# Layer 1's front as a pipeline over four steps, and layer 0's token totals placed behind later products

## The chip, the cores and the metric

The kernel runs on one core of one Trainium2 chip. The metric is the device time of one execution in microseconds; lower is better. A core has five engines that run side by side, each through its own queue of instructions in order: TensorE (PE, matrix products; its weight loads are shown apart as PEld), VectorE (DVE), ScalarE (ACT), GpSimd (POOL) and SyncE (SP), which here issues most of the DMA transfers. GpSimd issues the gathers, DMA transfers whose rows are picked by a list of indices.

## The reference

Four layers run one after the other on 2048 tokens of 512 numbers. Each layer mixes a token block with a per-request 64x64 matrix (or a like condition) and then runs a network; the result is added to x. The change touches the fronts of the first two:

```python
x = x + _L0_ffn_ref(_L0_cond_ref(x, ...), ...)   # attention, shared expert, 7 experts, the best 2 of each token
x = x + _L1_ffn_ref(_L1_cond_ref(x, ...), ...)   # 32 experts, the best 4 of each token
...
# layer 0, the experts
shared = expert_ffn(x, sh_gate, sh_up, sh_down)
probs = jax.nn.sigmoid(x @ router_w + router_b)
scores, idx = jax.lax.top_k(probs, 2)
...
return shared + combined
# layer 1, mixing and the choice of experts
w = weights[subjects]
out = jnp.einsum('bct,bcd->bdt', x, w)
...
logits = x @ gate_w.T + gate_b
topk_logits, topk_idx = jax.lax.top_k(logits, 4)
```

## The kernel before

The 2048 tokens are 16 tiles (`NT`) of 128 rows. Everything is float32 apart from small one-hot tables.

**Layer 0's front** (`layer0`, `Front`) runs 16 steps. In each, the list `turns` (L465) calls the stages in a fixed order, each for the tile that lies `lag` steps back, and `g.held` pins all instructions in that order on every engine. Two tiles at a time are entered in the lists of their experts by `Moe.put` (L1152), a generator with five parts: one-hot marks on VectorE; two products `at` on TensorE; places on VectorE; two float16 tables `a_` and `b_` (the second of two scalings is on ScalarE); and `total` (L1140), four products of the tables on TensorE and an add into `tokens` on VectorE. `front` (L863) runs parts one, three and four; `count` (L871) runs part two in odd steps and the total in even ones. After `count` come `down_rows` (the shared expert's second product), a few small stages, `qkv` and `probs_turn`.

The shared expert of tiles 6 to 12 (`LATER`) isn't done in layer 0's front. Two of these (`GAP`) are done between layer 0's experts and layer 1; the other five, tiles 8 to 12, fill TensorE during layer 1's front.

**Layer 1's front** (`Mixed.run`, L1780) finishes layer 0 and chooses layer 1's experts for each tile. For a tile: `fetch` gathers two expert rows `yk` per token (GpSimd); `adds` adds them, scaled, to x on VectorE (x of tiles 8 to 15 is loaded during the stage by `bridge.rest`); `mix` is a product with the tile's mixing matrix, copied to `c` by ScalarE and stored to `rows`; `turn` transposes c on TensorE and copies it to `cT` on ScalarE; `route` makes the logits, either in four parts on disjoint columns of the array (`SPLIT` tiles, with `partss` copied by ScalarE and summed by one more product in `logits`) or in eight products straight to `rp`; `choose` adds the bias and finds the largest values on VectorE. After tiles 3, 7, 11, 13 and 15 (`GROUPS`) a `Ranked.put` (L1504) of four or two tiles runs through five parts: VectorE, TensorE (`at`), VectorE, VectorE, TensorE (`table`).

The five shared experts are cut by `Shared.pieces` (L539) into 30 pieces: four quarters of gate and up for each tile (eight products of 128 columns), and two halves of down (one 512-column product each). When the fourth quarter is out, `act` on VectorE is kept as a late action that `acts` calls. After the second half of down, ScalarE copies the result to `sht` and GpSimd adds it to x.

In one step s of 17, the order written out by hand is: fetch(s + 6), mix(s), adds(s + 1), a piece, logits(s - 1), turn(s), late actions, choose(s - 1), a piece, the puts' next parts, route(s), a piece, a new put. So mix, turn and route of one tile follow each other on TensorE in one step, with one piece between each two. Four pieces stand ahead of step 0, and 26 in steps 0 to 8. Two PSUM buffers (tag `sh`) serve gate/up and down in turn, so a new gate/up buffer waits for the act of the tile before.

After the stage, `m.end` turns the table into the list `fixed`, by which the first expert rows are gathered for layer 1's experts.

Of the kernel before, what the change touches and what calls it, by code (L numbers as in the profile page):

```python
# [10 lines left out]
F32 = mybir.dt.float32  # L11
# [10 lines left out]
P = 128  # L22
# [19 lines left out]
FIXED1 = 2  # L42
TC1 = 96
LATER = range(6, NT - 3)
LEAD = 6
GROUPS = {3: 4, 7: 4, 11: 4, 13: 2, 15: 2}
SPLIT = range(9)
GAP = 2
EARLY = range(LATER[GAP])
BIG = 65536.0  # L50
# [374 lines left out]
def layer0(g, w3, pool3):  # L425
    tc, nc, a = g.tc, g.nc, g.a
    with ExitStack() as ctx:
        keep = ctx.enter_context(tc.tile_pool(name="l0keep", bufs=1))
        g.constants(keep, "cst01")
        clear = g.results(keep)  # L430
        xs = g.stream("x0")
        ln2 = g.load(keep, "ln2")
        m = Moe(g, ctx, keep, E0, K0, [C0] * E0, V0, "w_e0", W0, l0_expert, ln2)
        with ExitStack() as c1:
            wp = c1.enter_context(tc.tile_pool(name="l0w", bufs=1))
            sb = c1.enter_context(tc.tile_pool(name="l0sb", bufs=2))
            at0 = g.cond_rows(wp, "cond0")
            x, other = {}, {}

            def load(i):  # L440
                if i < NT:
                    x[i] = g.load_x(sb, a["x"], i, 5)

            def swapped(i):
                if i < NT:
                    other[i] = sb.tile([P, D], F32, name="xw")
                    for k in range(2):
                        r = i * P + 64 * (1 - k)
                        g.dma(other[i][64 * k : 64 * k + 64, :], a["x"][r : r + 64, :], later=False)

            load(0)
            swapped(1)
            load(1)
            load(2)
            w = {k: g.load(wp, k) for k in ("ln1", "w_lat", "w_q", "w_kn", "w_kr", "w_v", "w_o", "w_r0")}
            shared = Shared(g)
            w.update(shared.w)
            br = g.load_bcast(wp, "b_r0")
            g.at1 = g.cond_rows(wp, "cond1")
            ps = c1.enter_context(tc.tile_pool(name="l0ps", bufs=3, space=PSUM, reuse_waits="tile"))  # L460
            bank = ps.tile([P, 512], F32, name="tok", tag="tok", bufs=1)
            m.begin(sb, bank, bank[:, 256:448])
            f = Front(g, sb, ps, w, br, ln2, at0, m, x, other, xs, shared)

            turns = (  # L465
                ("mix", 0), ("copied", 0), ("values", 2), ("pair_scaled", 0), ("qk_turn", 1), ("pair_normed", 0),
                ("copied", -1), ("route", 3), ("out_turn", 2), ("gate_up", 3), ("norm_turn", 0), ("scores", 1),
                ("chosen", 3), ("pair_scaled", -1), ("latents", 0), ("softmax", 1), ("pair_normed", -1), ("weights", -2),
                ("front", 3), ("out", 2), ("summed", 2), ("count", 3), ("down_rows", 3), ("weigh", 1), ("scaled", 2),
                ("normed", 2), ("x_sum", 2), ("down_sum", 3), ("qkv", 0), ("probs_turn", 1), ("out_norm", 2),  # L470
            )
            plain, g.nc = g.nc, SimpleNamespace(**{**vars(g.held), "sync": g.nc.sync})
            for step in range(NT):
                if step:
                    clear()
                if step == 15:
                    m.weights(0)
                for stage, lag in turns:
                    if 0 <= step - lag and (lag >= 0 or step % 2 == 0):
                        getattr(f, stage)(step - lag)  # L480
                load(step + 3)
                if step % 2:
                    swapped(step + 2)
            m.weights(1)
            f.tail()
            m.end(sb)
            g.nc = plain
        m.ready(ctx)
        tot = keep.tile([P, NT], F32, name="tot0")
        nc.vector.tensor_reduce(tot, m.vals[:, :, 0:K0], AX.X, ALU.add)  # L490
        nc.vector.reciprocal(tot, tot)
        nc.vector.tensor_tensor(
            m.gates, m.vals[:, :, 0:K0], tot.unsqueeze(2).to_broadcast([P, NT, K0]), ALU.mult
        )
        w3["sb"] = ctx.enter_context(tc.tile_pool(name="l3p", bufs=1))
        bridge = Bridge(g, xs, shared)
        combined = m.run(xs, Side(g, (layer3_ahead(g, pool3, w3), bridge.work(), layer3_tables(g, w3)), w3))
        with ExitStack() as c2:
            sb = c2.enter_context(tc.tile_pool(name="gapsb", bufs=2, reuse_waits="tile"))
            ps = c2.enter_context(tc.tile_pool(name="gapps", bufs=2, space=PSUM, reuse_waits="tile"))  # L500
            todo = LATER[:GAP]
            for i in todo:
                shared.up(sb, ps, i)
            for i in todo:
                shared.down(ps, i, bridge.x[i])
        m.beyond()
        return bridge, combined


class Shared:  # L510
# [28 lines left out]
    def pieces(self, sb, ps, todo, x):  # L539
# [23 lines left out]
        def down(i, ic):  # L563
            if ic == 0:
                ys[i] = ps.tile([P, D], F32, name="y", tag="sh")
            nc.tensor.matmul(ys[i], acts[i][:, ic, :], w["w_shd"][:, ic, :], start=ic == 0, stop=ic == 1)
            if ic:
                t = sb.tile([P, D], F32, name="sht", bufs=2)
                nc.scalar.copy(t, ys[i])
                nc.gpsimd.tensor_tensor(x[i], x[i], t, ALU.add)  # L570

        on_pe = []
        for k, i in enumerate(todo):
            for q in range(4):
                if q == 2 and k:
                    on_pe += [(partial(down, todo[k - 1], ic), None) for ic in range(2)]
                on_pe.append((partial(up, i, q), partial(act, i) if q == 3 else None))
        on_pe += [(partial(down, todo[-1], ic), None) for ic in range(2)]
        return on_pe

    def down(self, ps, i, x, tag="sh"):

# [9 lines left out]
class Front:  # L592
# [276 lines left out]
            next(self.puts[0])  # L869

    def count(self, i):  # L871
        if self.puts:
            next(self.puts[0], None)
            if i % 2 == 0:
                self.puts.clear()

    def up(self, i, quarters):

# [835 lines left out]
class Mixed:  # L1714
# [17 lines left out]
    def adds(self, i):  # L1732
        if i >= NT:
            return
        g, x = self.g, self.bridge.x[i]
        for k, yk in enumerate(self.yk.pop(i)):
            g.held.vector.scalar_tensor_tensor(x, yk, self.before.gates[:, i, k : k + 1], x, ALU.mult, ALU.add)
        g.held.sync.dma_start(out=self.xs[i * P : (i + 1) * P, :], in_=x)

    def mix(self, i):  # L1740
        nc = self.g.held
        o = self.ps.tile([P, D], F32, name="mm", bufs=1)
        nc.tensor.matmul(o, self.bridge.weights[i], self.bridge.x[i], start=True, stop=True)
        self.c[i] = self.sb.tile([P, D], F32, name="c")
        nc.scalar.copy(self.c[i], o)
        nc.sync.dma_start(out=self.m.rows[i * P : (i + 1) * P, :], in_=self.c[i])
# [33 lines left out]
    def run(self):  # L1780
# [8 lines left out]
                self.late.pop(0)()  # L1789

        def fill(n=1):
            for piece, late in pieces[:n]:
                if len(pieces) <= 2:
                    acts()
                piece()
                if late:
                    self.late.append(late)
            del pieces[:n]

        def go(engine, among=None):  # L1800
            for put in list(puts if among is None else among):
                if put[1] == engine:
                    put[1] = next(put[0], None)
                    if put[1] is None:
                        puts.remove(put)

        for i in range(LEAD):
            self.fetch(i)
        fill(4)
        self.adds(0)  # L1810
        for s in range(NT + 1):
            self.fetch(s + LEAD)
            bridge.rest(self.wp, todo[0] + 2 + s)
            if s < NT:
                self.mix(s)
            if s not in SPLIT:
                go("tensor", puts[-1:])
            self.adds(s + 1)
            fill()
            if s:  # L1820
                self.logits(s - 1)
            if s < NT:
                self.turn(s)
            acts()
            if s:
                self.choose(s - 1)
            fill()
            go("tensor")
            go("vector")
            if s == NT - 1:  # L1830
                go("vector")
            if s < NT:
                self.route(s)
            fill()
            if s - 1 in GROUPS:
                puts.append([m.put(self.sb, self.ps, s - GROUPS[s - 1], GROUPS[s - 1]), "vector"])
                go("vector")
            if s in (10, 12):
                m.weights((s - 10) // 2)
        for engine in ("tensor", "vector", "vector"):  # L1840
            go(engine)
        gates = m.softmax()
        next(gates)
        go("tensor")
        assert not puts and not pieces
        m.end(self.ps)
        next(gates, None)

# [1102 lines left out]
```

## Time and profile before

| | us |
|---|---|
| median of 3 runs | 2548.62 (2548.58 to 2551.81) |
| the profiled execution | 2554.14 |
| its span, first to last instruction | 2552.3 |
| layer 0's front | up to about 362 |
| layer 0's experts and the two shared experts in the gap | to 589 |
| layer 1's front, to the token list | 589.8 to 706.1 |
| gathers `yk` in it | 32 issues, 589.95 to 661.3 |
| VectorE's scaled add of one gathered row block (128x512), median | 0.75 |
| ScalarE's copy of 128x512 | 0.59 |
| GpSimd's add of 128x512 to x | 1.27 |

A row of the timeline gives the start, the time that the merged instructions took, the engine, the line (L244 is the helper through which all pinned instructions go), the operation with the tile it writes and those it reads, the shape, and in brackets how long the engine had stood idle and what ended that. "issue" means that nothing in the profile explains the idle time, "remote" that a semaphore ended it whose sender the profile doesn't tell. A row of the waits gives an engine and tile, what it waited for, the total, how often, and the longest. Small differences of one profile (some tenths of a microsecond) are not to be read as time of the kernel.

### The profile page before, as it was taken

The numbers are of one execution on the slowest core, as the hardware profiler recorded it, in microseconds if no ns is written. First come the engines' busy times: TensorE is split into PE (matmuls) and PEld (weight loads), VectorE is DVE, ScalarE is ACT, GpSimd is POOL, SyncE is SP. The second block draws the span as 40 slices with busy tenths as digits, with TensorE's granted clock in tenths as the row PEclk, the third lists the DMA queues.
The fourth block names the chain that finished last, engine by engine and source line by source line (L and its number), as shares of the span: only waits on it lengthen the run. The fifth ranks groups of instructions, "written<-read, shape, count | busy, mean of one in ns | idle before, by whom it ended". The sixth has DMA issues, their size and how long they took to land.

```text
span 2552.3 us, 42553 instructions
## 1 busy us (share of the span) xinstructions
PE 2428.8 (95%) x16625; PEld 1622.7 (64%) x16625; DVE 1425.7 (56%) x3471; ACT 710.5 (28%) x1475; POOL 889.8 (35%) x928
## 2 busy tenths in 40 slices
PE   7999989998789999969999999999999999979998
PEld 5777766666566666747666666666666665435665
DVE  4667865733755554436544544544544432657897
ACT  2444511112211111101322222222222221246664
POOL 2122235604144443523333333333333212573440
PEclk8999999998799999989999999999999999989999
DMA  6242135526466977844222222222222213423551
GB/s 252 100 144 98 56 115 179 193 94 198 164 201 225 361 265 259 293 138 163 68 75 77 73 73 73 73 73 78 76 77 76 81 55 136 164 70 107 150 144 55
DMA packets 133850, 341.49 MB, mean 134 GB/s; under 512 B 24250, under 2 KB 25306, under 8 KB 126337
## 3 DMA queue, kind: packets, MB, share of 16 engines
q1 hardware_dynamic: 92000, 190.94, 21.7%
q0 software_dynamic: 41056, 141.89, 17.7%
q10 hardware_dynamic: 576, 5.77, 0.6%
q8 instruction: 136, 2.23, 0.4%
q14 instruction: 82, 0.66, 0.1%
HBM read 247.33 MB, written 107.22 MB: 139 GB/s over the span
## 4 chain that ended last, share of the span: by engine, by line
PE 51%; DVE 2%; POOL 1%; issue 1%; DMA 1%; ACT 0%; ACTq 0%; POOLq 0%; DVEq 0%; SPq 0%
PE out L2322 9%; PE lp L2181 8%; PE zp L2258 8%; PE pp L2637 3%; PE hp L2290 3%; PE gp L2313 3%; PE y L2886 2%; PE yp L2124 2%; PE sp L2816 2%; PE pT L2838 2%; PE op L2864 2%; PE ep L2267 1%; PE kp L2789 1%; PE out L2328 1%; PE ap L2112 1%
## 5 line engine op out<-in xcount | busy, mean ns | idle before, releaser
L1375 PE MATMUL gu<-xT,wt 128*128 128x320 f32 (+5 forms) x1536 | 397.5, 406 | 8.3 <-DVE xT L1362 7.0
L1375 PEld LDWEIGHTS gu<-xT,wt 128*128 128x128 f32 x1536 | 283.4, 192 | 121.9 <-issue 49.6
L2181 PEld LDWEIGHTS lp<-xnT,sb_mu 128*128 128x128 f32 x2048 | 236.3, 194 | 10.8 <-issue 6.7
L2181 PE MATMUL lp<-xnT,sb_mu 128*128 128x128 f32 x2048 | 239.3, 277 | 3.6 <-DVE xnT L334 2.9
L2322 PE MATMUL out<-sb_w,gT 128*128 128x512 f32 x512 | 234.9, 602 | 0.0
L2258 PE MATMUL zp<-sb_w,xnT 128*128 128x512 f32 x512 | 226.5, 592 | 0.0
L1388 PE MATMUL y<-wt,hT 128*128 128x512 f32 (+2 forms) x544 | 200.0, 595 | 1.2 <-DVE hT L1022 0.6
L362 POOL DMA_INDIRECT kvst<-kv,gidx x96 | 95.7, 997 | 263.7 <-DMA oldkv<-kvst 195.1
L2258 PEld LDWEIGHTS zp<-sb_w,xnT 128*128 128x128 f32 x512 | 93.7, 190 | 104.8 <-issue 102.4
L2322 PEld LDWEIGHTS out<-sb_w,gT 128*128 128x128 f32 x512 | 92.2, 190 | 96.1 <-issue 92.8
L362 POOL DMA_INDIRECT yk<-ys,slot x96 | 98.4, 1025 | 126.3 <-DVE pre L1484 82.0
L362 POOL DMA_INDIRECT kvt<-newkv,oidx x96 | 100.3, 1045 | 113.7 <-PE pT L2838 46.6
L2317 DVE COPY gT<-gp 128x512 f32<-128x512 f32 x64 | 44.3, 692 | 168.3 <-PE gp L2313 168.3
L1388 PEld LDWEIGHTS y<-wt,hT 128*128 128x128 f32 (+2 forms) x544 | 72.7, 166 | 63.9 <-issue 49.3
L362 POOL DMA_INDIRECT xr<-rows,stok x101 | 98.3, 973 | 37.6 <-issue 18.6
L1021 POOL TENSOR_TENSOR ga<-ga,sg 128x288 f32<-128x288 f32 (+5 forms) x66 | 50.9, 771 | 168.4 <-ACT sg L1017 167.0
L2295 ACT ACTIVATE h<-hp 128x512 f32<-128x512 f32 x128 | 73.1, 597 | 120.0 <-PE hp L2290 105.5
L2219 POOL TENSOR_TENSOR eT<-eT,inv 128x512 f32<-128x512 f32 x64 | 67.1, 1051 | 76.2 <-DVE inv L2218 70.3
L2269 ACT COPY ew<-ep 128x512 f32<-128x512 f32 x64 | 37.2, 583 | 201.9 <-PE ep L2267 201.9
L244 POOL TENSOR_TENSOR rstd<-ms,sb_cst 128x1 f32<-128x1 f32 x32 | 17.7, 554 | 210.6 <-DVE ms L244 210.6
L2186 DVE TENSOR_TENSOR lT<-lp,cmu 128x512 f32<-128x512 f32 x64 | 44.2, 690 | 81.0 <-PE lp L2181 79.1
L2827 ACT ACTIVATE s<-s,m 128x336 f32<-128x336 f32 x128 | 72.7, 569 | 46.7 <-DVE m L2823 39.4
(450 smaller groups left out, 4624.6 us busy)
## 6 DMA issues: line engine op xcount, KB each, us to landing
ys<-yo SPq DMA_DIRECT2D x106, 256.0 KB
oldkv<-kvst SPq DMA_DIRECT2D x96, 224.0 KB
kvt<-oldkv SPq DMA_DIRECT2D x96, 224.0 KB
ys<-zero SPq DMA_DIRECT2D x10, 2048.0 KB
xt<-x SPq DMA_DIRECT2D x62, 256.0 KB
x<-xt SPq DMA_DIRECT2D x48, 256.0 KB
wt<-w_e SPq DMA_DIRECT2D x7, 1536.0 KB
sb_w<-w SPq DMA_DIRECT2D x5, 1024.0 KB
```

Of the source, the lines that this page charges most:

```text
L362: ins = self.nc.gpsimd.indirect_dma_start(out=out, out_offset=None, in_=src, in_offset=bass.IndirectOffsetOnAxis(ap=idx, axis=0), **kw)
L1375: follow(nc.tensor.matmul(o, wj[:, c, ic * P : (ic + 1) * P], xTs[u][:, c, 0:n], start=c == 0, stop=c == 3))
L1388: follow(nc.tensor.matmul(y[row : row + n, :], hTs[e][:, ic, col : col + n], wd[:, ic, :], start=ic == 0, stop=ic == 1,))
L2181: g.first(e + c, nc.tensor.matmul(lp[:, e, :], w["mu"][:, c, (4 * q + e) * P : (4 * q + e + 1) * P], self.xnT[:, c, :], start=c == 0, stop ...
L2219: g.pin(nc.gpsimd.tensor_tensor(e3, e3, inv.unsqueeze(2).to_broadcast([P, 8, T]), ALU.mult))
L2258: g.first(c, nc.tensor.matmul(zp, self.xnT[:, c, :], w["w1"][:, c, cols], start=c == 0, stop=c == 3))
L2290: g.first(e + b, nc.tensor.matmul(hp[:, b, e, :], self.ews[q][r, e, :], self.z[q][r, e * P : (e + 1) * P], start=True, stop=True))
L2295: g.pin(nc.scalar.activation(self.hs[q][b], hp[:, b], AF.Gelu))
L2313: g.first(e + b + k, nc.tensor.matmul(gp[r, e, cols], self.hs[q][b][:, e, r], self.lT[q][:, e, cols], start=True, stop=True))
L2322: g.first(e, nc.tensor.matmul(self.out, self.gTs[q][:, e, :], w["w2"][:, 4 * q + e, :], start=False, stop=q + e == 6 and q == 3))
L2637: nc.tensor.matmul(pp, xT[i][:, c, :], (w["w_kv3"] if z else wq)[:, c, :], start=c == 0, stop=c == 3)
L2827: nc.scalar.activation(p, p, AF.Exp, bias=m, scale=-1.0, accum_out=tot)
```

## The change

In layer 0 the total leaves `count` and becomes a stage of its own, `tabled`, placed after `qkv`. In layer 1's front, step s now works on four tiles: mix(s), turn(s - 1), route(s - 2), and logits and choose(s - 3); there are 18 steps. `FILL` says how many pieces each step has (26 in steps 0 to 11). The parts form of the logits covers tiles 0 to 11. The shared experts' sums are added to x by VectorE straight from PSUM, as late actions. Gathers run three tiles ahead, with eight buffers for 14. The store of x moves from `adds` to `mix`.

```diff
-LEAD = 6
+LEAD = 3
 GROUPS = {3: 4, 7: 4, 11: 4, 13: 2, 15: 2}
-SPLIT = range(9)
+SPLIT = range(12)
+FILL = (2, 3, 2, 3, 2, 3, 2, 3, 2, 2, 1, 1)
...
-                ("normed", 2), ("x_sum", 2), ("down_sum", 3), ("qkv", 0), ("probs_turn", 1), ("out_norm", 2),
+                ("normed", 2), ("x_sum", 2), ("down_sum", 3), ("qkv", 0), ("tabled", 3), ("probs_turn", 1), ("out_norm", 2),
...
             nc.tensor.matmul(ys[i], acts[i][:, ic, :], w["w_shd"][:, ic, :], start=ic == 0, stop=ic == 1)
-            if ic:
-                t = sb.tile([P, D], F32, name="sht", bufs=2)
-                nc.scalar.copy(t, ys[i])
-                nc.gpsimd.tensor_tensor(x[i], x[i], t, ALU.add)
+
+        def add(i):
+            nc.vector.tensor_tensor(x[i], x[i], ys.pop(i), ALU.add)
+
+        def downs(i):
+            return [(partial(down, i, 0), None), (partial(down, i, 1), partial(add, i))]
...
     def count(self, i):
-        if self.puts:
+        if i % 2:
+            next(self.puts[0])
+
+    def tabled(self, i):
+        if i % 2 == 0 and self.puts:
             next(self.puts[0], None)
-            if i % 2 == 0:
-                self.puts.clear()
+            self.puts.clear()
...
-        g.held.sync.dma_start(out=self.xs[i * P : (i + 1) * P, :], in_=x)
 
     def mix(self, i):
-        nc = self.g.held
+        nc, x = self.g.held, self.bridge.x[i]
+        nc.sync.dma_start(out=self.xs[i * P : (i + 1) * P, :], in_=x)
...
         def fill(n=1):
+            acts()
             for piece, late in pieces[:n]:
-                if len(pieces) <= 2:
-                    acts()
                 piece()
...
-        for s in range(NT + 1):
+        for s in range(NT + 2):
             self.fetch(s + LEAD)
             bridge.rest(self.wp, todo[0] + 2 + s)
+            n = FILL[s] if s < len(FILL) else 0
+            if 3 <= s and s - 3 in SPLIT:
+                self.logits(s - 3)
             if s < NT:
                 self.mix(s)
-            if s not in SPLIT:
-                go("tensor", puts[-1:])
+            if s >= 3 and s - 3 < NT - 2:
+                self.choose(s - 3)
             self.adds(s + 1)
-            fill()
-            if s:
-                self.logits(s - 1)
-            if s < NT:
-                self.turn(s)
-            acts()
-            if s:
-                self.choose(s - 1)
-            fill()
+            fill(min(n, 1))
+            if 1 <= s <= NT:
+                self.turn(s - 1)
+            fill(max(n - 2, 0))
             go("tensor")
             go("vector")
-            if s == NT - 1:
-                go("vector")
-            if s < NT:
-                self.route(s)
-            fill()
-            if s - 1 in GROUPS:
-                puts.append([m.put(self.sb, self.ps, s - GROUPS[s - 1], GROUPS[s - 1]), "vector"])
-                go("vector")
+            if s >= 3 and s - 3 < NT - 2:
+                group(s - 3)
+            if s >= 2:
+                self.route(s - 2)
+            fill(min(n - 1, 1) if n else 0)
             if s in (10, 12):
                 m.weights((s - 10) // 2)
-        for engine in ("tensor", "vector", "vector"):
-            go(engine)
+            if s == NT:
+                self.choose(s - 2)
+                go("tensor")
+                go("vector")
+        self.choose(NT - 1)
+        group(NT - 1)
+        go("tensor")
+        go("vector")
+        go("vector")
```

`group(i)` starts the put that ends with tile i, as the loop did before.

More of the change, by code (lines that the diff above doesn't have):

```diff
@@ L575, in pieces @@
                 if q == 2 and k:
-                    on_pe += [(partial(down, todo[k - 1], ic), None) for ic in range(2)]
+                    on_pe += downs(todo[k - 1])
                 on_pe.append((partial(up, i, q), partial(act, i) if q == 3 else None))
-        on_pe += [(partial(down, todo[-1], ic), None) for ic in range(2)]
-        return on_pe
+        return on_pe + downs(todo[-1])
     def down(self, ps, i, x, tag="sh"):
@@ L1737, in adds @@
             g.held.vector.scalar_tensor_tensor(x, yk, self.before.gates[:, i, k : k + 1], x, ALU.mult, ALU.add)
-        g.held.sync.dma_start(out=self.xs[i * P : (i + 1) * P, :], in_=x)
     def mix(self, i):
-        nc = self.g.held
+        nc, x = self.g.held, self.bridge.x[i]
+        nc.sync.dma_start(out=self.xs[i * P : (i + 1) * P, :], in_=x)
         o = self.ps.tile([P, D], F32, name="mm", bufs=1)
-        nc.tensor.matmul(o, self.bridge.weights[i], self.bridge.x[i], start=True, stop=True)
+        nc.tensor.matmul(o, self.bridge.weights[i], x, start=True, stop=True)
         self.c[i] = self.sb.tile([P, D], F32, name="c")
@@ L1798, in fill, with go @@
             del pieces[:n]
-        def go(engine, among=None):
-            for put in list(puts if among is None else among):
+        def go(engine):
+            for put in list(puts):
                 if put[1] == engine:
@@ L1805, in go, with group @@
                         puts.remove(put)
+        def group(i):
+            if i in GROUPS:
+                puts.append([m.put(self.sb, self.ps, i + 1 - GROUPS[i], GROUPS[i]), "vector"])
+                go("vector")
         for i in range(LEAD):
@@ L1810, in run @@
         self.adds(0)
-        for s in range(NT + 1):
+        for s in range(NT + 2):
             self.fetch(s + LEAD)
             bridge.rest(self.wp, todo[0] + 2 + s)
+            n = FILL[s] if s < len(FILL) else 0
+            if 3 <= s and s - 3 in SPLIT:
+                self.logits(s - 3)
             if s < NT:
                 self.mix(s)
-            if s not in SPLIT:
-                go("tensor", puts[-1:])
+            if s >= 3 and s - 3 < NT - 2:
+                self.choose(s - 3)
             self.adds(s + 1)
-            fill()
-            if s:
-                self.logits(s - 1)
-            if s < NT:
-                self.turn(s)
-            acts()
-            if s:
-                self.choose(s - 1)
-            fill()
+            fill(min(n, 1))
+            if 1 <= s <= NT:
+                self.turn(s - 1)
+            fill(max(n - 2, 0))
             go("tensor")
             go("vector")
-            if s == NT - 1:
-                go("vector")
-            if s < NT:
-                self.route(s)
-            fill()
-            if s - 1 in GROUPS:
-                puts.append([m.put(self.sb, self.ps, s - GROUPS[s - 1], GROUPS[s - 1]), "vector"])
-                go("vector")
+            if s >= 3 and s - 3 < NT - 2:
[3 more added lines that the diff above has]
+            fill(min(n - 1, 1) if n else 0)
             if s in (10, 12):
                 m.weights((s - 10) // 2)
-        for engine in ("tensor", "vector", "vector"):
-            go(engine)
+            if s == NT:
[6 more added lines that the diff above has]
+        go("vector")
+        go("vector")
         gates = m.softmax()
@@ L1844, in run @@
         go("tensor")
-        assert not puts and not pieces
+        assert not puts and not pieces and not self.late
         m.end(self.ps)
```

## The prediction

> **What bounds the kernel now.** I read the page first. Over the whole program TensorE is nearly always busy, so what can be won lies where it is not; layer 1's front (about 590 to 706 us) lies in the tenth and eleventh slices (63.8 us each), where PE falls to 8 and 7 tenths.
>
> ```profile
> span 2552.3 us, 42553 instructions
> PE   7999989998789999969999999999999999979998
> DVE  4667865733755554436544544544544432657897
> ```
>
> Next I asked for busy time by windows over that front. The columns after the window are its length, then PE, PEld, DVE, ACT and POOL busy (number of instructions), the granted clock, the DMA share and GB/s.
>
> ```profile
> 589.80:706.10 116.30, 91.02 (x514) 65.32 (x514) 72.28 (x203) 28.74 (x54) 38.92 (x37) 0.79 0.60 194
> 595.70:697.50 101.80, 83.60 (x458) 58.72 (x459) 64.75 (x178) 26.81 (x51) 34.38 (x33) 0.78 0.63 206
> 605.40:619.10 13.70, 8.93 (x40) 7.09 (x41) 3.30 (x8) 3.00 (x6) 9.15 (x9) 0.50 0.74 221
> 660.00:673.70 13.70, 11.40 (x44) 7.86 (x44) 10.89 (x31) 2.51 (x5) 1.90 (x2) 0.50 0.74 250
> ```
>
> VectorE has 72 us of work in 116 us and PE 91, part of it at a granted clock of 0.50. Neither fills the stage: it is a chain that hops between engines. The stage starts with the first mix product (595.7) and what ends it is the last choice of experts (697.3), from which another 8.8 us lead to the token list (706.05). The waits name the hops:
>
> ```profile
> ACT c L244 <- PE mm L244: 28.5, 13, 3.9
> POOL xt L244 <- ACT sht L244: 20.5, 4, 7.3
> DVE lg L244 <- remote: 8.8, 1, 8.8
> ACT partss L244 <- remote: 6.1, 1, 6.1
> ```
>
> The two "remote" waits, and one of 3.0 us before a cT copy at 641, are hold-ups: in the timeline the product that fed `partss` ended at 599.4, yet ScalarE began at 604.97, and the next two links also came late.
>
> ```profile
> 604.97 0.27 ACT L244 COPY partss<-parts 128x128 f32<-128x128 f32 x1 [6.13 <-remote]
> 609.18 0.59 ACT L244 COPY c<-mm 128x512 f32<-128x512 f32 x1 [3.95 <-issue]
> 612.71 0.19 DVE L244 TENSOR_TENSOR lg<-rp,bc_b_r 128x32 f32<-128x32 f32 x1 [8.77 <-remote]
> ```
>
> From 597 to 604 DMA moved 321 GB/s, a share of 0.98. After each such pause PE got half the clock, above. For layer 0's front PE's waits between 40 and 355 us tell all: 304.9 of 315 us busy, and one wait that repeats.
>
> ```profile
> PE tok L244 <- ACT a L244: 4.3, 6, 0.9
> ```
>
> **Layer 0.** `tabled` moves six totals (four 128x35 products and one DVE add of 0.18 us each) behind down_rows and qkv. Those take PE from 122.1 to 128.0 in the step that I looked at, while the wait is at most 0.89 us, so the operands are there. What lies behind the total is probs_turn, whose exponentials ended at 120.6; `tokens` now queues on DVE behind the rotation (to 129.1), before a copy that starts at 129.16, at 0.2 us a step. Since PE has no other idle time to absorb it, 4.3 us come off; with a few tenths returned to that copy I count **-4.0** (bounds -4.3 and -2).
>
> **Layer 1, prices.** At full clock, start to start: mix 0.86 us, one quarter of gate/up 0.90, one down half 0.86, transposes 0.46, split logits 0.35 and their sum 0.14, one tile's unsplit logits 0.90, `at` 0.55, a table of four tiles 1.9. DVE: two scaled adds 1.53, choose 0.72, gate-up's act 0.89, one put of four tiles 2.55 + 2.1 + 3.1.
>
> **Sums on VectorE.** Five adds of 0.68 us (layer 0's same add lasts 675 ns) replace five 0.59 us copies and five 1.27 us POOL adds. DVE gains 3.4 us of work, but four of those POOL adds lay beside DVE instructions that were long for it: pairs of scaled adds of 1.92, 2.50 and 2.56 us for 1.53, and one `sel` of 1.32 for 0.29, together 3.4 us. Net 0. POOL's 20.5 us behind `sht` vanish, hidden anyway, for the gathers were early.
>
> **Gathers three ahead.** 32 issues of 0.95 us remain, 1.25 us apart. Buffers go from 14 to 8, so a gather waits for the add four tiles back. A gather lands 4 to 5 us after issue; three steps are over 12 us. In the first 20 us POOL issues back to back in either form, so the DMA burst stays, and adds of tiles 2 to 4 still wait for it. 0, bounds 0 and +3. SP: x's store moves from adds to mix, and so waits for nothing that isn't done; 0.
>
> **The pipeline.** Four stages now belong to four tiles, so PE no longer waits for the copy of c or cT it has just caused; what is queued behind PE's waits now is DVE's work. I laid the new order out on the two engines with the prices above, zero at the first mix. Steps 0 to 2 follow the gathers: step 3 starts at 12.6. In steps 3 to 11 the PE sums are 4.4, 3.6, 4.5, 3.6, 5.1, 3.5, 5.5, 2.7, 3.2, in all 36; DVE has 2.3, 2.9, 3.1, 5.5, 5.2, 5.4, 2.9, 5.7, 5.0, in all 38. A new gate/up accumulator needs the act of the tile before, which sits on DVE behind choose and the two adds: PE waits 2.7 us for it in step 5, 3.1 in 7, 2.6 in 10, and 1.0 for the first table. Step 12 starts at 12.6 + 36 + 9.4 = 58. From there DVE sets the pace: it is 2.5 us behind, has 24.6 us of puts, choices and adds in steps 12 to 17, and waits some 1.2 for `at`; the last choice begins at 86. PE's sparse steps at half clock (as now after 660) add 2: **88**.
>
> The old order laid by the same prices, with its last seven steps as measured (41.4 us), also gets there at 88; measured are 101.6. So the order by itself is worth about nothing, and the 13.6 us between are the hold-ups and the half clock that follows them. What the pipeline buys is distance: at the first one PE has mix 1, both down halves, three gate/up quarters and mix 2, some 7 us of products, that need nothing ScalarE makes late, where it now stood for 3.1 and 4.0 us. Bounds of what stays of the 13.6: 0 and all. I take 7, by the 4.0 us in which it must still wait for c(1) and 3 for the clock that falls after it: 88 + 7 = 95, against 101.6 **-6.6**.
>
> The two more steps at the end are in the 24.6 us. The tail from the last choice to the token list keeps its 8.8; its extra table (1.9) lies under the last choose and put.
>
> Sum: -4.0 - 6.6 = -10.6. The profiled execution spans 2552.3 (2554.1 with what lies around it), 5.5 above the median 2548.6; the difference applied to the median gives **2538**.
>
> **The rivals.**
> *A, PE starves and loses its clock (slower).* The three waits on DVE's act are as long as the pauses after which the clock fell: 1.5 us before 660.0, 1.9 before 643.0. If they bring 0.50 from step 5 to step 11, PE's 28 us there become 56 in 38 us of schedule: +18, so 2556. It turns the sign once half clock holds for over three fifths of those steps (10.6 of 18). For it: the 13.7 us that one fall lasted. Against: the old order was 5.8 of 8 busy at 652 to 660, less than the new one would be. [...] The rows here show falls after 1.5 us, so A stays in.
> *B, the hold-ups come back whole.* They belong to the DMA burst, which is unchanged, and the order is worth nothing: only layer 0 is left, 2544.6. For it: 88 against 88.
> *C, they vanish.* If distance covers all of them, 88 against 101.6: -13.6 - 4 = 2531. For it: PE's own 7 us of cover against pauses of 3 to 4.
> *D, the gathers don't do what is said:* with eight buffers one comes late at each early add, +3 for the first five tiles and the cover gone: 2547.
>
> **How the numbers follow.** Forecast 0.42, C 0.25, B 0.18, A 0.10, D 0.05. A measurement of this kernel tells 0.2%, 5.1 us, from no change. Faster by that needs 2543.5 or less: all of C, nearly all of the forecast, a part of B, 0.71. Within it B's rest and D, 0.18; slower A with a mishap of the forecast's cover, 0.11. The range reaches from C less some 4 us by which my laying may be off, 2527, up to 2550, which leaves out A alone; the likeliest case alone holds 2533 to 2543.
>
> **What would show it.** In the new profile: no PE wait for ACT `a` at tok in layer 0 (4.3 gone); in layer 1's front no `c <- PE mm` wait that PE then waits for; PE waits for DVE `hT` of 2 to 3 us in three or four places; first mix to last choice 95 us; no POOL tensor instruction there; a granted clock over the front above 0.79. Wrong it would be if PE stands on `remote` or late links as long as before (B), if the clock is 0.5 through steps 5 to 11 (A), or if DVE adds wait for yk landings after the fifth tile (D).

## The result, and the profile after

The changed kernel takes 2537.14 us (median of six runs, 2530.74 to 2540.64), the kernel before 2549.11 (six runs, 2547.74 to 2551.81). The ratio is 0.9948, 95% interval 0.9934 to 0.9963: 12.0 us less between the medians. The profiled execution after spans 2536.2 us against 2552.3, 16.1 less: the profile of before is of an execution (2554.14 us) 5.0 us over the median, that of after (2537.99) of one 0.9 over its own. Of the 16.1 us, 2.3 lie ahead of layer 0's token counts, 2.8 between these and the first mix, which the change does not touch, 10.8 in layer 1's front from first mix to last choice, and 0.2 behind it.

The page after, first its span and then the two rows of busy tenths that were shown of before:

```profile
span 2536.2 us, 42559 instructions
PE   7999989998699999969999999999999999979998
DVE  4667865834755544436454444454454432658887
```

PE's slices ten and eleven still dip (8 and 6 for 8 and 7): the front ends earlier but is no fuller. Below, busy time by windows over the front after, cut at four marks: first mix, fourth mix (step 3), thirteenth mix (step 12), last choice of experts. The last row is the whole. Columns as in the prediction.

```profile
590.56:609.41 18.85, 14.60 (x69) 10.17 (x69) 6.62 (x11) 3.77 (x8) 12.05 (x12) 0.76 0.89 288
609.41:653.11 43.70, 40.72 (x274) 27.39 (x274) 33.29 (x94) 13.76 (x30) 19.44 (x16) 0.95 0.77 253
653.11:681.37 28.26, 19.68 (x123) 15.08 (x123) 23.58 (x79) 6.71 (x12) 0.00 (x0) 0.78 0.49 159
590.56:681.37 90.81, 74.99 (x461) 52.64 (x462) 63.50 (x183) 24.23 (x50) 31.49 (x28) 0.86 0.71 231
```

The same cut of the kernel before:

```profile
595.71:622.13 26.42, 18.55 (x101) 13.30 (x102) 9.12 (x20) 5.29 (x11) 16.61 (x17) 0.74 0.82 258
622.13:675.02 52.89, 46.10 (x276) 31.62 (x274) 38.35 (x100) 15.55 (x31) 17.76 (x16) 0.84 0.59 199
675.02:697.29 22.27, 18.73 (x84) 13.58 (x84) 17.11 (x57) 5.97 (x9) 0.00 (x0) 0.69 0.47 163
```

From first mix to last choice 101.6 became 90.8. The first stretch gave 7.6 us and the second 9.2; the third took 6.0 back. The marks do not cut the two orders at the same work: behind the thirteenth mix the new one still has 123 products, the old one 84, and ahead of the fourth it has 69 for 101. The first stretch, laid out at 12.6, still took 18.9. The waits in the front after say why:

```profile
ACT c L245 <- PE mm L245: 23.6, 14, 3.6
PE table L245 <- DVE a L245: 9.0, 4, 3.7
ACT c L245 <- remote: 8.1, 1, 8.1
DVE xt L245 <- remote: 7.8, 1, 7.8
PE mm L245 <- ACT c L245: 3.8, 1, 3.8
PE y L245 <- DVE hT L245: 2.1, 1, 2.1
```

The "remote" waits are the hold-ups of before again. In the timeline after, the product of mix 1 was done at 594.6 by PE's record, its copy began at 600.73, and PE then stood before mix 2, as the tile `mm` has one buffer:

```profile
593.45 1.10 PE L245 MATMUL mm<-xt,wbd 128*128 128x512 f32 x2
...
600.73 0.58 ACT L245 COPY c<-mm 128x512 f32<-128x512 f32 x1 [8.13 <-remote]
...
601.37 1.22 PE L245 MATMUL mm<-xt,wbd 128*128 128x512 f32 x1 [3.77 <-ACT c L245]
```

In layer 0, of PE's waits between 40 and 355 us after, the old wait of `tok` for `a` is gone. Three lines of what is left are these:

```profile
PE ap L245 <- DVE sT L245: 0.9, 2, 0.6
PE mix L245 <- DVE sT L245: 0.7, 3, 0.2
PE tok L245 <- DVE lg L245: 0.3, 1, 0.3
```

PE is busy in 308.0 of these 315 us where it was in 304.9 (3.4 us of them, from 334.3, at half clock), and layer 0's token counts come at 360.5 instead of 362.8. Before, the wait for `sT` ahead of `ap` was 0.2, and none ahead of `mix` is listed.

### The profile page after: what moved, and what is told of

Same layout as the page of the kernel before. It is cut to its first block, busy times and chain, and to the rows that moved or that the text cites. A ratio compares the mean times of both kernels' runs of the same rounds, so it can differ in the third digit from the quotient of the medians.

```text
span 2536.2 us, 42559 instructions
## 1 busy us (share of the span) xinstructions
PE 2415.5 (95%) x16616; PEld 1614.4 (64%) x16631; DVE 1421.7 (56%) x3476; ACT 706.4 (28%) x1473; POOL 883.3 (35%) x923
## 4 chain that ended last, share of the span: by engine, by line
PE 50%; DVE 3%; issue 1%; POOL 1%; DMA 1%; ACT 0%; SPq 0%; ACTq 0%; POOLq 0%; DVEq 0%
PE out L2333 9%; PE lp L2192 8%; PE zp L2269 8%; PE pp L2648 3%; PE hp L2301 3%; PE gp L2324 3%; PE yp L2135 2%; PE y L2897 2%; PE sp L2827 2%; PE pT L2849 2%; PE op L2875 2%; PE ep L2278 1%; PE kp L2800 1%; PE ap L2123 1%; PE out L2339 1%
## 5 line engine op out<-in xcount | busy, mean ns | idle before, releaser
L2192 PEld LDWEIGHTS lp<-xnT,sb_mu 128*128 128x128 f32 x2048 | 234.8, 193 | 10.8 <-issue 6.7
```

The source lines that it names most:

```text
L2192: g.first(e + c, nc.tensor.matmul(lp[:, e, :], w["mu"][:, c, (4 * q + e) * P : (4 * q + e + 1) * P], self.xnT[:, c, :], start=c == 0, stop ...
```

## The experiments

Two theories stood at first. One: the pipeline's distance between an operation and what needs it covers the hold-ups. The other: the order within a step, with no wait for the copy just caused, carries the gain. A third came up on the way: the number of gathers that GpSimd issues in a row sets the hold-up, so the short lead carries the gain.

Twelve kernels ran on three chips, four on each, each time beside the kernel before, whose medians there were 2547.83, 2549.54 and 2526.93 us. Single executions of one kernel lie up to 22 us apart, and each ratio has an interval of some 3 to 5 us either way; so the stretches of the profiles are read beside the times. But a profile is of one execution only.

**Layer 0's part alone, and all but it**

```
 before + ("qkv", 0), ("tabled", 3), ("probs_turn", 1)   with count/tabled of after
 after  - ("tabled", 3)                                  with count of before
```

> The kernel before with the layer 0 part alone: the even tiles' token totals go behind the next tile's products, layer 1's front as before. Prediction on record: -4.0 us (bounds -4.3, -2). The profile after speaks for less: the wait of 4.3 us is gone, yet layer 0's front ends only 2.3 us earlier, so now -2 to -3. Rival (all of it is given back at the copies on VectorE): 0, within 1 us of the kernel before. The front of layer 1 should keep its 101.6 us from first mix to last choice in either case.

> The changed kernel with layer 0's totals put back where they were: layer 1's pipeline, sums and lead alone. If the two parts add up, this and the run of the layer 0 part together give the 12 us of the whole: -9 to -10 here. First mix to last choice 91 us as after (101.6 before). Rival (the layer 0 part shifts the phase of layer 1's start and that is what shortened the hold-up there): above -6, with the first three steps over 22 us again.

Layer 0's part alone: ratio 0.9993 (0.9974 to 1.0012). All but it: 0.9985 (0.9969 to 1.0002), 4.4 us less by the median where 9 to 10 were expected, with a front of 94.8 us. The parts do not visibly add up to the 12 us; the intervals allow it only near their ends. The token counts came at 359.8 us in both profiles, with the part and without it. The front of the first took 107.7, with one hold-up of 14.3 us, so the size of a hold-up differs from one profile to the next with the same order and lead (26.4 us and 30.3 in the first stretch). These two runs point to less than the 4.0 counted for layer 0's part; the interval of the first, -6.6 to +3.1 us, does not exclude it.

**The lead put back, and the sums put back**

```
 after  -LEAD = 3
        +LEAD = 6
 after  -nc.vector.tensor_tensor(x[i], x[i], ys.pop(i), ALU.add)
        +nc.scalar.copy(t, ys[i]); nc.gpsimd.tensor_tensor(x[i], x[i], t, ALU.add)
```

> The changed kernel with the lead of the gathers put back to six tiles (14 buffers for 8). Prediction on record: the lead is worth 0 (bounds 0 and +3 for the short lead), so the same as after, ratio 0.995 to before, and VectorE's waits for yk after the fifth tile under 1 us in both. Rival: the short lead thins the burst of transfers at the start and so shortens the hold-up; then this one is 3 to 6 us slower than after, with first mix to step 3 near 26 us as before (18.9 after).

> The changed kernel with the shared sums put back: ScalarE copies the product, GpSimd adds it (five copies of 0.59 us and five adds of 1.27 us for five VectorE adds of 0.68). Prediction on record: net 0 for the sums, so within 1.5 us of after. Rival: the sums on VectorE carry a good part of the gain, as GpSimd's adds stretch VectorE's scaled adds and hold back the gathers queued behind them: 3 to 5 us slower than after.

With the long lead most of the gain is gone: 0.9991 (0.9974 to 1.0008), 2.5 us less by the median. With the old sums it stays: 0.9969 (0.9953 to 0.9984), 8.5 less. But all of the change except layer 0's part, which has the short lead, gave 4.4 on this same chip, so these runs alone do not settle what the lead is worth. The windows of the kernel with the long lead, cut as above:

```profile
587.42:615.11 27.69, 13.72 (x69) 9.16 (x69) 6.72 (x11) 3.28 (x7) 17.58 (x18) 0.73 0.79 254
615.11:659.53 44.42, 41.34 (x274) 28.15 (x274) 33.24 (x94) 13.70 (x30) 11.35 (x10) 0.94 0.67 220
```

The second stretch is that of the pipeline (43.7 after), the first that of the kernel before (26.4). In it PE did 13.7 us of work in 27.7. Its timeline shows a hold-up from the inside. The columns are start, time, engine and operation, and in brackets the idle time before it; "issue" means that it waited for nothing that the profile shows:

```profile
593.33 1.05 PE L245 MATMUL gu<-hnT,sb_w_sh 128*128 128x128 f32 x8
...
602.49 1.24 PE L245 MATMUL gu<-hnT,sb_w_sh 128*128 128x128 f32 x3 [1.92 <-issue]
605.27 0.37 PE L245 MATMUL gu<-hnT,sb_w_sh 128*128 128x128 f32 x1 [1.54 <-issue]
606.68 0.37 PE L245 MATMUL gu<-hnT,sb_w_sh 128*128 128x128 f32 x1 [1.04 <-issue]
607.39 0.58 PE L245 MATMUL gu<-hnT,sb_w_sh 128*128 128x128 f32 x1 [0.33 <-issue]
608.81 0.37 PE L245 MATMUL gu<-hnT,sb_w_sh 128*128 128x128 f32 x1 [0.85 <-issue]
610.22 0.37 PE L245 MATMUL gu<-hnT,sb_w_sh 128*128 128x128 f32 x1 [1.04 <-issue]
614.64 0.63 PE L245 MATMUL rp<-sb_cst,partss 128*128 128x32 f32 x2 [4.05 <-ACT partss L245]
```

Its waits have the line of ScalarE that goes with it:

```profile
ACT c L245 <- remote: 13.6, 1, 13.6
```

The eight products of one quarter took 1.05 us at 593; eight of a later quarter took 8.1, from 602.49 to 610.6, and worked in 3.3 of them, with nothing named that they wait for. Whether PE lacked operands or its own instructions the profile does not tell. Of the 14.0 us that PE stood in the first stretch, 4.1 are a wait by name, for `partss`, since ScalarE had stood for 13.6 us before its next copy. The rest has no name: here PE itself crawls, and the order of the work could have covered little of it.

A long first stretch does not make a slow execution by itself. This profile is of the second fastest of its twelve executions (2539.70 us, median 2545.30). That with the old sums, with a first stretch of 14.6, is of the third slowest of its twelve (2543.45, median 2539.34).

**The short lead alone**

```
 before -LEAD = 6
        +LEAD = 3
```

> The changed kernel itself once more, on one chip with the next three, since single executions of one kernel lay up to 19 us apart in the runs before this. Expected: 8 to 13 us below the kernel before. First mix to step 3 between 15 and 20 us in its profile (18.8 and, in the two other runs with the short lead, 20.4 and 14.6).

> The kernel before with nothing changed but the lead of the gathers, three tiles for six. New theory: the hold-ups follow GpSimd's back-to-back gathers; a lead of six issues 14 of them in a row, one of three only 8, and that is worth 6 to 8 us in the first three steps (26.4, 30.3 and 27.7 us with the long lead in three profiles; 18.8, 20.4, 14.6 with the short). Then this runs 5 to 8 us below before, with first mix to step 3 under 22 us. Prediction on record (lead worth 0, bounds 0 and +3): the same as before or up to 3 us slower. Third theory (only pipeline and short lead together pay): within 1 us of before, though the first three steps shorten.

The changed kernel again: 0.9959 (0.9944 to 0.9975), 9.2 us less. The kernel before with this one number changed: 0.9971 (0.9956 to 0.9986), 7.8 us less. Its profile is of the fastest of its twelve executions (2535.08, median 2541.76), so its stretches flatter it. Its windows:

```profile
592.12:609.18 17.06, 13.98 (x101) 10.08 (x102) 9.64 (x20) 5.20 (x11) 11.11 (x11) 1.00 0.83 275
609.18:657.09 47.91, 40.91 (x276) 28.28 (x274) 38.15 (x100) 15.81 (x32) 23.77 (x22) 0.96 0.71 235
657.09:677.97 20.88, 17.33 (x84) 12.49 (x84) 17.02 (x57) 5.97 (x9) 0.00 (x0) 0.75 0.68 253
```

The old order with the short lead has a shorter front than the changed kernel, 85.9 us for 90.8, and a first stretch of 17.1 with the clock at 1.00. The edit costed at nothing is the largest part of the gain on this chip; the 1.5 us between the two runs lie within the noise.

How the lead does it is not shown. A lead of six has 14 buffers and one of three 8, but that is not the number of gathers in a row, as the expectation had it, since the adds free buffers meanwhile. In the traces the first row of gathers without a pause (starts up to 2.2 us apart) is 16 long before, 14 after, 16 in the changed kernel again and 10 in the old order with the short lead. Sixteen in a row go with a first stretch of 26.4 us before and of 19.2 in the changed kernel again. So the length of the row alone does not set the hold-up.

**A lead of two, and the scalings on ScalarE**

```
 after  -LEAD = 3
        +LEAD = 2
 and    -nc.vector.tensor_scalar(a_[:, j], a_[:, j], tok, None, ALU.mult)
        +nc.scalar.activation(a_[:, j], a_[:, j], AF.Copy, scale=tok)
```

> The changed kernel with the lead cut once more, to two tiles: 6 gathers in a row at the start for 8, and 6 buffers. If the hold-ups grow with the run of gathers, first mix to step 3 falls to 13 to 17 us and the whole to 1 to 4 us below after. Rival: a gather now starts only two steps ahead, and as it lands 4 to 6 us after its issue and some steps take 3 to 4 us, VectorE's adds wait for it in most steps: over 3 us slower than after.

> As the run before it, and the 16 scalings of a_ by the token numbers (0.25 us each) go from VectorE to ScalarE. VectorE was busy 7.1 and 7.6 of 8 us in some of the last steps after, ScalarE 25.8 of 106. If VectorE sets the end of the front, it falls 2 to 4 us against the run before it (the last stretch from mix 12 to the last choice, 28 us, shortens). Rival: the scaled a_ comes later from ScalarE than from VectorE and the tables on TensorE wait for it: 0 to +3.

The lead of two gives 0.9944 (0.9925 to 0.9964, six runs), a front of 88.5 us, but a first stretch of 18.6, no shorter than with three. Its interval overlaps that of the changed kernel beside it. With the scalings on ScalarE the gain shrinks to 0.9978 (0.9963 to 0.9994), and the second stretch grows from 41.6 to 50.4. The groups of its front tell why:

```profile
L245 ACT ACTIVATE a<-a,sb_cst 128x384 f16<-128x384 f16 x12 | 6.4, 603 | 8.3 <-DVE a L245 8.3
L245 PE MATMUL rp<-sb_cst,partss 128*128 128x32 f32 x24 | 4.7, 281 | 11.7 <-ACT partss L245 10.6 <-DVE sg L245 0.7 <-issue 0.4
```

A scaling takes 603 ns on ScalarE (316 in the median on VectorE, in the profile after), and it waits there for VectorE's `a`, 8.3 us in all. Copies of `partss` stand behind it in ScalarE's queue, and PE waits 10.6 us for them (1.8 without this edit). An engine that is often idle (ScalarE was busy in 24.2 of the 90.8 us of the front after) is not free for such work, if what others need stands behind it in its queue, as `partss` did here.

**The old order with the short leads; six spare gathers; the lead of two again**

```
 before + layer 0's part, LEAD = 3        before + layer 0's part, LEAD = 2
 after  +if s == 0: 6 x g.gather(spare, ys, slot[:, i, k])   behind the fetch of tile 3
```

> The kernel before with the short lead of three and the layer 0 part, but layer 1's old order and GpSimd's sums: the change without its pipeline. The short lead alone gave 8.0 us (interval of some 3.4 either way) and a front of 85.8 us against 90.8 to 94.8 with the pipeline. If the order is worth nothing or less, this is as fast as the changed kernel or faster: -9 to -14, front 84 to 90 us. Rival (the pipeline adds 3 to 5 us to the short lead, as 11.3 against 8.0 would have it): 2 us or more slower than after, -5 to -9.

> As the run before it with a lead of two tiles: 6 gathers in a row at the start. If the run of gathers sets the hold-up, 1 to 3 us below it (-10 to -16), first three steps 14 to 17 us. Rival: the old order adds a tile right after the mix before it, so a gather two steps ahead comes late in the short steps and VectorE waits for yk: 2 us or more above it.

> The changed kernel with six gathers more, issued in step 0 behind those of the fourth tile, into buffers that nobody reads: 14 gathers in a row as with a lead of six, the lead itself still three. If the run of gathers makes the hold-up, the first three steps grow from 19 to 25 to 30 us with waits that the profile puts to no engine (remote, or PE's products done and signalled late), and the whole loses 5 to 9 us against after. Rival (the lead acts through the number and place of the buffers): the first three steps stay at 15 to 20 us and the whole within 2 us of after. Third possibility: the real gathers of tiles 4 and 5 come late behind the spare ones, and VectorE waits for yk by name, 2 to 7 us; that would not speak for the first.

> The changed kernel with a lead of two again, beside the old order with a lead of two on one chip; six executions of it before gave -15.2 us (interval of some 3.4 either way). Expected -11 to -15. If the order is worth nothing, within 3 us of the old order with a lead of two; if the pipeline pays, 3 us or more below it.

In the order of the expectations: 0.9982 (0.9971 to 0.9994), 1.0007 (0.9993 to 1.0021), 0.9990 (0.9979 to 1.0001) and 0.9988 (0.9972 to 1.0004), by the medians 3.5 us less, 3.1 more, 0.7 less and 2.8 less. On this chip the kernel before is 21 to 23 us faster than on the two others, and the gains of 9 to 16 us that three of the expectations name did not come. None of the four profiles has a hold-up: they have no "remote" wait in layer 1's front. The window of the first stretch with the spare gathers:

```profile
586.45:598.50 12.05, 12.03 (x68) 8.96 (x69) 6.72 (x11) 3.48 (x7) 9.61 (x9) 0.86 0.93 300
```

That of the lead of two, and its whole front:

```profile
585.94:596.54 10.60, 10.60 (x69) 7.73 (x69) 6.03 (x10) 3.48 (x7) 8.16 (x9) 1.00 0.95 316
585.94:668.69 82.75, 71.69 (x461) 50.39 (x462) 63.52 (x183) 24.00 (x49) 31.34 (x28) 0.88 0.74 253
```

PE is busy in 12.03 of 12.05 and in 10.60 of 10.60 us, at a DMA share of 0.93 and 0.95. So on this chip heavy transfers alone do not hold PE up, and a long row of gathers does not either (26 without a pause, from 580.5 to 614.1, in the trace with the spare ones). What the spare gathers did was the third possibility, later rows for tiles 4 and 5, in the waits of that kernel:

```profile
DVE xt L245 <- DMA yk<-ys,slot: 12.7, 9, 7.1
```

Whether this longer row would have made the hold-up longer on one of the other chips was not tried: the run fell on a chip without hold-ups.

At a lead of two the order does make a difference in time: 2530.07 us for the old order and 2524.16 for the new one, 5.9 apart, where the last expectation had named 3 as the sign that the pipeline pays. From 565 to 625 us VectorE waits 7.8 us for `yk` in the old order and 4.9 in the new one (5.3 in the old order with a lead of three, 2523.46 us). But the profile does not put the loss there: the front of the old order takes 84.7 us with a lead of two and 90.2 with three, and it starts 5.3 us later, out of layer 0, where the two have the same code. The cause stays open.

The version that beats both kernels was not found with certainty either. The lead of two is the best by its median on the second chip (14.9 us less), and 2.8 us less on the third, within its interval of nothing.

**What the records themselves say.** Each product of PE that signals its end was set beside the next semaphore event of PE on record. In the median the event comes 0.014 us after the product's end. Between 350 and 690 us, on the first two chips and in the first two profiles, it comes up to 5.8 us after it near 365, up to 6.9 near 495 and up to 13.5 near 600 (in the profile after also up to 4.3 near 438, at six products); on the third chip none is over 1 us late there. Some of these events may be missing and not late: the ten profiles of the first kind hold 1853 to 1868 of them for some 1,980 products, the four of the third chip 1979 to 1982. The ten also have fewer records of landed transfers, in all and from 587 to 604 us:

```
                                     landings recorded   late groups
                                      in all  587-604    350 to 690 us
 before                               14981      61      at 3 places
 after                                14768      68      at 4 places
 lead of six, new order               14649      53      at 3 places
 lead of three, old order             14655     112      at 3 places
 lead of two, new order               14617      88      at 3 places
 old order, lead 3 (third chip)       18090     357      none
 old order, lead 2 (third chip)       18088     288      none
 spare gathers (third chip)           18187     335      none
 lead of two, new order (third chip)  18083     361      none
```

Eight of the ten profiles with fewer records have "remote" waits of 4.0 us or more in layer 1's front up to 625 us, the longest 14.3 (the changed kernel again and the scalings on ScalarE have none); the four with more records have none, and all four are of one chip. So fewer records and hold-ups come together as far as these profiles go. Which is the cause of the other, or whether something else disturbs both, no run here shows.

## Why the prediction was right, and where it was not

The time came out (2538 forecast, 2537.1 measured), within the likeliest case's own range; the division behind it did not hold. That the sum fits is luck: the 6.6 us that it gave to the pipeline came, as far as the runs show, for the most part from the short lead, which it had put at nothing.

*Gathers three ahead: 0, bounds 0 and +3.* This is the step that failed. It said that "in the first 20 us POOL issues back to back in either form, so the DMA burst stays", and from that concluded no effect. The premise held (16 gathers without a pause before, 14 after); the conclusion did not. Measured: the short lead alone gave 7.8 us (interval 3.6 to 11.2) on one chip, and the change without it 2.5 (-2.0 to 6.6) on another; the whole change gave 9.2 beside the first of these and 12.0 in the pair of the result. On the first two chips and the chip of the first profiles the first stretch took 26.4, 30.3 and 27.7 us with a lead of six in three profiles, and 14.6 to 20.4 with a lead of three in five, whichever the order. The bound left out a gain, and there was no reason in the profile that excluded one: the row that the prediction itself had, hold-ups just where GpSimd issues without pause, was the hint. By what the lead acts stays open.

*The pipeline: -6.6 by distance.* The first half, "the order by itself is worth about nothing", agrees with the profiles. Both orders were laid at 88 us; of the new one's, 75.4 lie from step 3 on (88 less 12.6). Measured from step 3 to the last choice are 68.8 to 77.4 us in five profiles of the old order (mean 73.7), and 69.9 to 77.9 in eight of the new one (mean 73.3; the run with the scalings on ScalarE left out). The times of the two orders at a lead of two, 5.9 us apart, are the one result against it. The second half fell: with the long lead the pipeline's first stretch still takes 27.7 us, so its cover buys nothing there. In that profile it could buy little, since PE itself crawled. The 7 us that were to stay, by the wait for c(1), were 6.2 (18.85 less 12.6), with a wait of 3.77 us before mix 2 in it; but by the profile with the long lead half of the hold-up had gone with the lead, not with the order. Without hold-ups the laid front of 88 was measured at 82.8 with a lead of two and at 89.6 with the spare gathers.

*Layer 0: -4.0.* The mechanism held, the size did not. The 4.3 us of waits are gone, but the end comes 2.3 us earlier in the pair of profiles: waits for the copy `sT` went from 0.2 to 1.6 us, where "a few tenths" had been allowed for them, and 3.4 us at half clock came with them. In the profiles of the first two chips and the first pair, the token counts come at 362.8, 359.8 and 360.9 us without the part (mean 361.2) and at 359.3 in the mean of seven with it (356.8 to 363.0): 1.9 us, less than single profiles scatter. The timed run alone allows anything from -6.6 to +3.1.

*Sums on VectorE: net 0.* Not refuted: with the old sums the kernel keeps 8.5 us by its median on one chip, and the changed one 9.2 on another.

*The rivals.* A did not come: the clock was 0.95 from step 3 to step 12, and the one wait for `hT` was 2.1 us, with 3.4 us of half clock from 644.9 on. The longest wait at the end, 3.68 us for `a` up to 674.9, came with half clock from 672.2 on for 27.3 us; the tables there had been slow in the old order too (0.69 in its last stretch, 0.78 now). B, the hold-ups whole, is what the lead of six showed; C, no hold-ups, is what the third chip showed. So in these profiles B and C follow the lead and the chip, and not the order. D did not come: waits for yk were 3.0 us in all after.

*The signs.* Right were the wait of `tok` gone, no GpSimd tensor work in the front, and a higher clock (0.86 from first mix to last choice, 0.78 before). Wrong were 95 us (90.8), "no c<-mm wait that PE then waits for" (one of 3.8; mix 2 had been counted as cover, though its one buffer makes it wait for the copy of mix 1), and three or four waits for `hT` (one; PE's waits in the steps at the end were for the puts' `a`, 9.0 us in four).

## What to carry to other kernels

Give every edit of a schedule that changes how far ahead transfers are issued a bound on both sides, and test it by itself first: here, on the chip where it was tried, one number, 6 to 3, held most of what a rewritten loop seemed to bring. A wait that the profile puts to no engine need not be slack that a better order can cover; look whether the engine that signals late was itself standing, as PE was with the long lead, at 8.1 us for eight products that had taken 1.05. And set a gain beside the same pair on another chip before it is called the kernel's: 9 to 12 us here were 3.5, 2.8, 0.7 and -3.1 for four near relatives of the changed kernel on a chip without the hold-ups, where the changed kernel itself was not run.

## What was not expected of the hardware

The kernel before took 2549.5 us on one chip and 2526.9 on another, by the medians. It has no profile on the faster chip, but the changed kernel with a lead of two has one on each: their spans are 2529.7 and 2521.2 us, 8.5 apart, and the first stretch alone is 18.6 and 10.6 us, 8.0 apart. Between 350 and 690 us PE's semaphore events are late by over 1 us or missing near 365, 495 and 600 (up to 5.8, 6.9 and 13.5 us), on the slower chips only. Near 365 and 495 that costs little: from the token counts to the first mix are 229.0 to 232.9 us there and 228.9 to 229.9 on the faster chip. Near 600 waits without a named cause last up to 14.3 us; in one profile, eight products took 8.1 us instead of 1.05. Landings of transfers are missing there from the records (88 left in 17 us for 361, in the two profiles of one kernel). A DMA share of 0.93 to 0.95 with PE at work without a gap, on the faster chip, shows that the transfers do not do it alone. What starts a hold-up, and whether it is there when nothing is recorded, stays open.
